# Delta-rule attention on one Trainium2 core: keys, decays and inverses of all heads in the front, the loop fed by one stream of products

## The chip, the cores and the metric

The kernel runs on one core of a Trainium2 chip, in float32. A core has five engines that run side by side, each with its own queue of instructions in a fixed order: TensorE (PE, with its weight loads PEld), VectorE (DVE), ScalarE (ACT), GpSimd (POOL) and SyncE (SP, which here only issues DMAs; ACT and POOL issue some too). The metric is the device time of one execution in microseconds (us), as the median of several runs. Lower is better.

## The reference, cut to what matters

Two layers work on x of 2 sequences x 1024 tokens x 512 channels. Only the first layer's attention is changed:

```python
xn = _layernorm(x)
q = silu(causal_dwconv(xn @ Wq, 4 taps)); k = ...Wk * 128**-0.5; v = ...Wv   # 16 heads of 128
alpha = sigmoid(xn @ Wa + ba); beta = sigmoid(xn @ Wb + bb)                  # one a head and token
# for each token, S is 128x128 for each head and sequence:
#   err = S k - v;  S = alpha * S - beta * err k^T;  o = S q
o = layernorm(o) * ln_w + ln_b
s = (o * sigmoid(xn @ Wg)) @ Wo
g = silu(ternary_swiglu(xn))
x = x + s * g
# second layer: a gated linear recurrence and an FFN of 4-bit weights, in the same manner
```

## The kernel before

**Tiling.** The recurrence over tokens is done in chunks of 128 tokens (NC = 8 a sequence). The 16 heads x 2 sequences make 32 streams, in 8 head groups (`hg`) of 4 streams (2 heads x 2 sequences). A unit is one chunk of one head group: 64 units in all, in the order of `units`: unit u is group 2(u // 16) + u % 2 and chunk (u % 16) // 2, so two groups are worked on side by side, and four such pairs of groups follow one another. The projections q, k, v and gate are made by pieces of two chunks (`p`, 4 a head group).

**Inside a chunk** the delta rule needs the inverse of a triangular matrix of 128 x 128 for each stream. Its diagonal blocks of 32 x 32 are inverted for a whole head group at once by `invert` (L836): blocks of all chunks and streams lie across the 128 partitions, and 31 steps of two tensor_tensor operations follow (`tl` the product, `ml` the subtraction), each on 31 to 256 elements a partition. The blocks come from and go to DRAM (`dl`, loads and stores on SP).

**Stages of `first_layer` (L311).**
1. Layernorm of the 16 token tiles and their transposes (xnT). The ternary FFN is a generator, `mlp()`, with 48 steps; `some(n)` takes n steps of it wherever it is called, so that its matmuls fill gaps.
2. The front, a Python loop over head groups 0 to 3 and their pieces. For each piece: `piece_k().direct` (projection of k by 8 matmuls 128x512, then the three later taps of the convolution as DVE operations with a halo of 3 tokens kept by POOL, and Silu on ACT), `ahead_e` (decays: rows loaded by DMA, a mask on DVE, exponentials on ACT, `e`), `ell()`, which calls `ahead_l` (matmuls `pkk` = k k^T, weighted with e on DVE to `lt`, eight small DMAs a piece to `dl`), and some steps of `invert` for the group before (groups 0 and 1 here). `x_sums` on POOL (`tx`) makes sums of xnT blocks that Strassen-Winograd products need, and two `some(1)` put FFN steps in each piece. The weights of k (`wk`) are loaded on SP at the head of each group.
3. A short prologue: q and v of the first pieces of groups 0 and 1.
4. The loop of 64 units. `weave` (L1240) lays out each unit by hand in 10 slots: in each slot one step of a chain (`across`, the recurrence of this unit and the end of the unit before), whatever `later(n, ...)` has put down for this slot in `due`, and then as many of the `others` as their share of PE work allows: `within` (decays and products inside the next chunk: pqk, kd), `finish` (layernorm of o), and the projections by Winograd with 7 steps a piece where the direct way takes 8, `Piece.step`. The order on each engine in the loop is that written order (`Ordered`, L126). `tasks(u)` (L1199) says which one or two pieces a unit makes: 7 or 14 steps. In the loop before, besides q, v and gate of all groups, k, decays and L of groups 4 to 7 and the inverses (on DVE) of groups 2 to 7 are made, and 11 half output projections (`half`, products `poh`, stored to `pd`).
5. `Join` (L142): the output projection by token tiles (`jpo`, 16 matmuls, or 8 where a half was made), gating with the FFN's output, layernorm, transposes. Then the second layer.

**Pieces in the loop.** After the products of a piece, `Piece.complete` (L730) evicts, adds the ends, applies the bias on ACT (`start`), then three taps for each of two halves on DVE and Silu on ACT. Each of these is put `later` in slots that follow. In `within` (L875) the decays of a unit are loaded to `eb` from DRAM; that tile has one buffer, and the load is issued one slot after the rest.

The front and the stages outside the loop are ordered by a scheduler when the program is built; in the loop the order is as written.

Of the kernel before, what the change touches and what calls it, by code (L numbers as in the profile page):

```python
# [22 lines left out]
P = 128  # L23
# [4 lines left out]
H = 16  # L28
# [113 lines left out]
class Join:  # L142
# [5 lines left out]
    def __init__(self, tc, a, cst, minus_half, od, gd, x1d, pd, room):  # L148
        self.tc, self.a, self.cst, self.minus_half = tc, a, cst, minus_half
        self.room = room.rearrange("p k b t -> p (k b t)")  # L150
        self.od, self.gd, self.x1d, self.pd, self.a = od, gd, x1d, pd, a
        self.ctx = ExitStack()
        self.tp = [self.pool("j_t", 1)]
        self.op = [self.pool("j_o", 1)]
        self.lp = self.pool("j_ln", 3)
        self.wo = []
        self.order = [(c, b) for c in range(NC) for b in range(B)]
        self.o, self.xg, self.made = [], [], 0
        self.load_xg()
# [17 lines left out]
    def load_o(self):  # L177

        n = len(self.o)
        c, b = self.order[n]  # L180
        ot = self.op[n % 3 > 0].tile([P, H, P], F32, tag="ot", name=f"jo_{b * NC + c}")
        h0 = 0
        if n in self.pd:
            h0 = H // 2
            self.tc.nc.sync.dma_start(ot[:, 0:4], self.pd[n].rearrange("p (k t) -> p k t", k=4))
        self.tc.nc.sync.dma_start(
            ot[:, h0:], self.od[c].rearrange("p (h b) t -> p b h t", b=B)[:, b, h0:]
        )
        self.o.append(ot)
# [12 lines left out]
    def product(self, psp, tag, matmul):  # L202
# [9 lines left out]
        h0 = H // 2 if i in self.pd else 0  # L212
        for h in range(h0, H):
            matmul(po, lhsT=ot[:, h, :], rhs=self.wo[h], start=(h == h0), stop=(h == H - 1))  # L214
            if h == H - 1:
# [14 lines left out]
                def gated():  # L230
                    total = po
                    if h0:
                        total = ot[:, 0:4].rearrange("p k t -> p (k t)")
                        nc.vector.tensor_tensor(total, total, po, ALU.add)
                    nc.vector.tensor_tensor(g, total, g, ALU.mult)
# [75 lines left out]
def first_layer(ctx, tc, a, cst, minus_half, keep, xnT, od, gd, pd, then):  # L311
# [32 lines left out]
    early = ctx.enter_context(ExitStack())  # L344
    pa = early.enter_context(tc.tile_pool(name="at_a", bufs=2))
# [165 lines left out]
    pl = early.enter_context(tc.tile_pool(name="at_l", bufs=1, reuse_waits="tile"))  # L511
    wab = pl.tile([P, KC, 2 * H], F32, name="wab")
# [84 lines left out]

    def mm(out, **kw):
        PE.matmul(out, **kw)
# [17 lines left out]
    class Piece:  # L617


        def __init__(self, n, hg, p, dst, after=None):  # L620
# [5 lines left out]
            else:  # L626
                self.pre = pools["p"].tile(
                    [P, 2, B, 2 * P + 4], F32, tag="pre", name=f"pre{self.u}",
                    bufs=3 if "b" in pools else 2,
# [11 lines left out]
        def direct(self, w):  # L641
# [13 lines left out]
            self.complete(0, False)  # L655


        def begin(self, w, x, both, urgent, spare):

            self.w, self.x, self.both, self.urgent = w, x, both, urgent  # L660
            self.engine = POOL if spare else DVE
# [11 lines left out]
        def ended(self):  # L673
            self.left -= 1
            if not self.left:
                self.complete(3 if self.n == "v" else 1, self.urgent)

        def end(self):

            self.ends -= 1  # L680
            if not self.ends:
                ends = self.out[:, 0:4:3]

                def add():
                    self.engine.tensor_tensor(ends, ends, self.both, ALU.add)
# [44 lines left out]
        def complete(self, n, urgent):  # L730
# [32 lines left out]
            if urgent:  # L763
                taps = [lambda a=a, b=b: (a(), b()) for a, b in zip(taps[0::2], taps[1::2])]
            later(
                n,
                lambda: (start(0), kept(), start(1)),
                *taps,
                lambda: (ACT.activation(dst, dst, AF.Silu), self.after()),
            )  # L770
# [40 lines left out]
    def ahead_l(hg, c, store):  # L811

        e, ka = store["es", c // 2][c % 2], store["ka", c // 2]
        k = ka[:, :, (c % 2) * P : (c % 2 + 1) * P]
        assert store["made", c // 2]
        pkk = pools["i"].tile([P, NS, P], F32, tag="pi", name=f"pkk_{hg}_{c}")
# [19 lines left out]
    def invert(hg, store):  # L836
# [14 lines left out]
        for i in range(31):  # L851
# [3 lines left out]
            DVE.tensor_tensor(  # L855
# [6 lines left out]
            DVE.tensor_tensor(rest, rest, tv, ALU.subtract)  # L862
# [12 lines left out]
    def within(hg, c, store):  # L875
# [6 lines left out]
        e = pools["b"].tile([P, NS, P], F32, tag="eb", name=f"eb_{u}", bufs=1)  # L882
# [4 lines left out]
        def block(s):  # L887
# [6 lines left out]
            lambda: nc.sync.dma_start(e, store["e"][c]),  # L894
# [175 lines left out]
    def ell():  # L1070
        if ls:
            hg, p = ls.pop(0)
            for c in (2 * p, 2 * p + 1):
                done(ahead_l(hg, c, stores[hg]))
                if c == 2 * p and hg == 0:
                    some(1)
# [21 lines left out]
    for hg in range(4):  # L1098
        stores[hg] = new_store(hg)
        wk = front_weights(hg)  # L1100
        steps = invert(hg - 1, stores[hg - 1]) if 0 < hg < 3 else iter(())
        for p in range(NP):
            for step in of_e:
                step()
            some(1)
# [3 lines left out]
            of_x = x_sums(n // 4, n // 2 % 2) if n % 2 == 0 else []  # L1109
# [5 lines left out]
            some(1)  # L1115
            ell()
            for _ in zip(range(0 if hg and not p else 14), steps):
                pass
# [6 lines left out]

    tc.keep_in_program_order(nc.vector.tensor_scalar(lnwb, lnwb, 0.5, None, ALU.mult))
# [56 lines left out]
    def piece(n, hg, p):  # L1183

        if n == "k":
            return piece_k(hg, p, stores[hg])
        dst = pools["b"].tile(
            [P, NS, 2 * P], F32, tag=n, name=f"{n}_{hg}_{p}", bufs=3 if n == "gate" else 2
# [4 lines left out]

    def x_of(n, hg, p):

        j = hg // 2 - 2 if n == "k" else hg // 2
        return xs[(NP * j + p) % 2]

    def tasks(u):  # L1199

        j, at = u // 16, u % 16
        p, A, C = at // 4, 2 * j, 2 * j + 1

        def after(hg):
            return (hg, p + 1) if p + 1 < NP else (hg + 2, 0)

        if u >= len(units) - 4:
            return [("gate", (A, C)[at % 4], p)] if u < len(units) - 2 else []
        found = (
            (("k", A + 4, p), ("gate", A, p)),  # L1210
            (("v", *after(A)), ("k", C + 4, p)),
            (("q", *after(A)), ("gate", C, p)),
            (("q", *after(C)), ("v", *after(C))),
        )[at % 4]
        return [t for t in found if t[1] < HG]
# [6 lines left out]
    def woven(pieces, beside):  # L1222

        if beside is none:
            for which, i in ORDER:
                if which < len(pieces):
                    pieces[which].step(i)
                    yield WIDE
        else:
            for i in (None, 0, None, None, 1, 4, None, 5, None, None, 2, 6, None, None, 3):  # L1230
                if i is None:
                    next(beside)
                else:
                    pieces[0].step(i)
                yield WIDE
            done(beside)
# [3 lines left out]
    def weave(chains, others):  # L1240
# [5 lines left out]
        for i in range(LINKS):  # L1246
            order["slot"] += 1
            next(chains[i % 2], None)
            for step in due.pop(order["slot"], ()):
                step()  # L1250
            while given < (i + 1) / LINKS * total:
# [5 lines left out]
    with tc.issue_after(last["act"].ins):  # L1257
        for g in range(2):
            done(step() for step in load_x(g, nc.gpsimd))
        for t in (("q", 0, 0), ("v", 0, 0), ("q", 1, 0), ("v", 1, 0)):  # L1260
            for steps in load_w(*t, nc.gpsimd):
                done(step() for step in steps)
        for i, t in enumerate((("q", 0, 0), ("v", 0, 0), ("q", 1, 0), ("v", 1, 0))):
            one = piece(*t).begin(weights[t], x_of(*t), boths[i % 2], False, True)
            for k in (0, 1, 4, 5, 2, 6, 3):
                one.step(k)
        done(within(0, 0, stores[0]))
        for t in tasks(0):
            for steps in load_w(*t, nc.gpsimd):
                done(step() for step in steps)  # L1270
        halves = sorted(pd)

        class half:


            wo = []

            @classmethod
            def more(cls):
                tag, n = ("e", 2) if cls.wo else ("ka", 2)  # L1280
                for _ in range(n):
                    h0 = len(cls.wo)
                    shape, k = ([P, NS, P + 4], 1) if tag == "e" else ([P, NS, 2 * P], 2)
                    w = pa.tile(shape, F32, tag=tag, name=f"woh_{h0}", bufs=4 if tag == "e" else 2)
                    w = w.rearrange("p s t -> p (s t)")[:, : k * D].rearrange("p (h e) -> p h e", h=k)
                    nc.sync.dma_start(
                        w, a["wo"][h0 * P : (h0 + k) * P, :].rearrange("(h p) e -> p h e", p=P)
                    )
                    cls.wo += [w[:, h, :] for h in range(k)]

            @classmethod
            def load(cls):
                c, b = halves[0] // B, halves[0] % B
                o = pools["w"].tile([P, 7, 2, P], F32, tag="w", name=f"oh_{halves[0]}")
                cls.o = o.rearrange("p k h t -> p (k h) t")[:, 0 : H // 2]
                nc.sync.dma_start(
                    cls.o, od[c].rearrange("p (h b) t -> p b h t", b=B)[:, b, 0 : H // 2]
                )

            @classmethod  # L1300
            def product(cls):
                i, o = halves.pop(0), cls.o
                po = pools["a"].tile([P, D], F32, tag="A", name=f"poh_{i}")

                def out():
                    part = pa.tile([P, NS, P], F32, tag="lt", name=f"part_{i}")
                    part = part.rearrange("p s t -> p (s t)")
                    ACT.copy(part, po)
# [654 lines left out]
```

## Time and profile before

| | us |
|---|---|
| median of 3 runs | 3325.73 (3321.27 to 3327.11) |
| the profiled execution | 3308.21 |
| its span | 3306.4 |
| layernorm, transposes, first FFN steps | 0 to 109 |
| front | 109 to 436 |
| prologue | 436 to 472 |
| loop, first to last unit (a unit begins with the DVE operation `rt`) | 472.5 to 1939.7 |
| output projection and join | 1940 to 2101 |
| second layer | 2101 to 3306 |

Busy over the span: PE 3112.5 us, DVE 2201.2, ACT 1420.0, POOL 1036.7. Times from the profile belong to the profiled execution; the runs' median is 17.5 us longer. A line of a window gives from:to, the length, the busy time and number of instructions of PE, PEld, DVE, ACT and POOL, the granted PE clock (1.00 is full), the busy share of the DMA engines and GB/s. A line of a tile gives line, engine, operation, output<-inputs, count, shortest/median/longest ns, first and last start, and forms (partitions x elements). A float32 matmul leaves two records. In names, the buffer numbers are left out; the timeline gives start, length, engine, line and operation, and in brackets the idle time before it and what ended it; the chain of work gives start, length and what ran. A line of the waits gives who waited for whom: us in total, times, longest.

### The profile page before, as it was taken

To read this page: it belongs to the slowest core of one execution; us is meant where nothing else is said; L and a number is where in the kernel's file an instruction comes from. 1 tells how busy PE (TensorE), PEld (TensorE's weight loads), DVE (VectorE), ACT (ScalarE), POOL (GpSimd) and SP (SyncE) were. 2 spreads that over 40 slices of the span, in tenths; PEclk is the share of its full clock that TensorE was granted. 3 is DMA by queue.
4 is the path that set the end of the run, shared out by engine and by line. 5 is a ranking of instruction groups with operands and counts; after the bars stand their busy time and mean duration, and the time that the engine had idled before them with its cause. 6 is when DMAs were issued, how large, how long until landed. Compare 5 with 4: busy or idle time off the path is not lost. (4 is left out here: it accounts for less than half of the span.)

```text
span 3306.4 us, 41655 instructions
## 1 busy us (share of the span) xinstructions
PE 3112.5 (94%) x13734; PEld 2236.5 (68%) x13734; DVE 2201.2 (67%) x4429; ACT 1420.0 (43%) x2646; POOL 1036.7 (31%) x1286
## 2 busy tenths in 40 slices
PE   8999978988988888899999899999999999999998
PEld 6566757877877777787888864455555555555554
DVE  5566747767677676656666547567667676766677
ACT  3476646655656556444454431132223222322223
POOL 2210053333533334333522222233323333333322
PEclk9999989998999989999999999999999999999999
DMA  7344486665776657565665548201001100011013
GB/s 211 98 139 118 120 253 209 185 190 170 224 217 184 186 171 221 176 189 176 212 181 182 173 140 256 85 32 32 26 26 32 32 26 27 25 39 32 26 35 128
DMA packets 523976, 428.69 MB, mean 130 GB/s; under 512 B 211440, under 2 KB 438512, under 8 KB 523760
## 3 DMA queue, kind: packets, MB, share of 16 engines
q1 hardware_dynamic: 404528, 281.55, 28.7%
q10 hardware_dynamic: 111648, 129.00, 12.6%
q0 software_dynamic: 7584, 15.47, 1.5%
q8 instruction: 110, 1.80, 0.2%
q14 instruction: 106, 0.87, 0.1%
HBM read 291.12 MB, written 122.16 MB: 125 GB/s over the span
## 5 line engine op out<-in xcount | busy, mean ns | idle before, releaser
L134 DVE TENSOR_TENSOR acc<-acc,po 128x512 f32<-128x512 f32 x408 | 278.3, 682 | 208.2 <-PE po L134 207.5
L134 PEld LDWEIGHTS po<-w_d,i 128*128 128x128 f32 x1024 | 194.5, 190 | 142.6 <-issue 110.3
L134 PE MATMUL po<-w_d,i 128*128 128x256 f32 (+1 forms) x1024 | 275.3, 392 | 0.0
L134 ACT COPY g<-pga 128x512 f32<-128x512 f32 x96 | 56.3, 587 | 447.5 <-PE pga L134 437.9
L134 PE MATMUL pga<-xq,w_g 128*128 128x512 f32 x512 | 240.7, 592 | 1.4 <-ACT g L134 1.4
L134 PE MATMUL pua<-xq,w_u 128*128 128x512 f32 x512 | 240.6, 592 | 0.0
L134 ACT ACT_TABLE_LOAD x171 | 219.4, 1283 | 30.5 <-PE pr L134 11.3
L134 POOL TENSOR_TENSOR rs<-rs,minus_half 128x4 f32<-128x4 f32 x64 | 81.7, 1276 | 398.9 <-DVE rs L134 326.2
L134 PEld LDWEIGHTS po<-w_d,s 128*128 128x128 f32 x720 | 136.8, 190 | 95.4 <-issue 77.0
L134 PE MATMUL po<-w_d,s 128*128 128x256 f32 x720 | 184.8, 379 | 0.0
L134 DVE SCALAR_TENSOR_TENSOR v<-prev,cw,v 128x512 f32<-128x512 f32 x192 | 166.6, 872 | 25.2 <-ACT v L134 24.0
L134 POOL TENSOR_TENSOR ot<-ot,gate 128x512 f32<-128x512 f32 x64 | 84.9, 1327 | 303.9 <-ACT ot L134 285.8
L134 DVE SCALAR_TENSOR_TENSOR ka<-prek,cw,ka 128x512 f32<-128x512 f32 x192 | 155.3, 812 | 35.8 <-ACT ka L134 34.2
L134 DVE TENSOR_TENSOR rr<-rr,zw 128x128 f32<-128x128 f32 x192 | 54.9, 286 | 181.3 <-PE zw L134 175.4
L134 PEld LDWEIGHTS pua<-xq,w_u 128*128 128x128 f32 x512 | 96.0, 190 | 76.8 <-issue 72.2
L134 ACT COPY w<-zw 128x128 f32<-128x128 f32 x192 | 51.0, 265 | 225.4 <-PE zw L134 198.0
L134 PE MATMUL paq<-xnT,wq 128*128 128x256 f32 x512 | 137.9, 393 | 10.1 <-ACT preq L134 10.0
L134 PEld LDWEIGHTS pga<-xq,w_g 128*128 128x128 f32 x512 | 97.2, 190 | 72.9 <-issue 66.7
L134 PE MATMUL pagate<-xnT,wgate 128*128 128x256 f32 x512 | 138.3, 395 | 8.7 <-ACT gate L134 8.2
L134 DVE SCALAR_TENSOR_TENSOR q<-preq,cw,q 128x512 f32<-128x512 f32 x192 | 140.2, 746 | 7.0 <-ACT q L134 4.9
L134 ACT ACTIVATE on<-po,nm,rs 128x128 f32<-128x128 f32 x256 | 103.1, 461 | 93.4 <-DVE nm L134 85.7
L134 PE MATMUL pqk<-q,kb 128*128 128x128 f32 x512 | 82.9, 313 | 64.0 <-DVE kd L134 63.6
(284 smaller groups left out, 7856.9 us busy)
## 6 DMA issues: line engine op xcount, KB each, us to landing
wv<-dwv ACTq DMA_DIRECT2D x24, 896.0 KB, 6.2
wq<-dwq ACTq DMA_DIRECT2D x24, 896.0 KB, 6.8
xnT<-dx ACTq DMA_DIRECT2D x42, 512.0 KB, 4.8
wgate<-dwgate ACTq DMA_DIRECT2D x24, 896.0 KB, 6.6
e<-gr SPq DMA_DIRECT2D x64, 256.0 KB, 4.7
de<-e SPq DMA_DIRECT2D x64, 256.0 KB, 3.3
dk<-ka SPq DMA_DIRECT2D x32, 512.0 KB, 3.1
kb<-dk SPq DMA_DIRECT2D x64, 256.0 KB, 3.5
```

Of the source, the lines that this page charges most:

```text
L134: i = getattr(self.engine, name)(*args, **kw)
```

## The change

- The front runs over all 8 head groups (32 pieces). A piece takes one FFN step instead of two (two in every sixth), the x sums come every fourth piece, and the L products alternate between two PSUM pools.
- `invert` gets its engine as an argument. In the front it is GpSimd, for groups 0 to 6, 14 steps at each of the pieces 1 to 3 of the next group. The inverse of group 7 is made on DVE in units 0 to 31, two steps a unit.
- The loop starts at u = −4 and has no k, decays or L. q, v and gate of both groups of a pair come from one stream, `woven()`, of 48 pairs of pieces x 14 steps; units take 10 or 11 steps of it up to unit 57, then 7, 5, 5 and 4. Units −4 to −1 have no chain and take the place of the prologue.
- Taps and Silu go to a list, `put_off`, of which each slot takes one (two if over 14 wait). The adds of the ends are always on POOL.
- `eb` has two buffers and its load is issued at once. q, v, gate and pre have 3, 2, 4 and 4 buffers (2, 2, 3 and 3 before).
- No half output projections: `jpo` has 16 matmuls for every tile. wo is loaded at units 60 and 62.

The diff, cut to its core:

```diff
-    def invert(hg, store):
+    def invert(hg, store, engine):
...
-            DVE.tensor_tensor(
+            engine.tensor_tensor(
                 tv,
...
-            DVE.tensor_tensor(rest, rest, tv, ALU.subtract)
+            engine.tensor_tensor(rest, rest, tv, ALU.subtract)
...
+    put_off = collections.deque()
+
+    def soon(*steps):
+        if order["loop"]:
+            put_off.extend(steps)
+        else:
+            done(step() for step in steps)
...
             taps = [functools.partial(tap, hl, i) for hl in range(2) for i in range(3)]
-            if urgent:
-                taps = [lambda a=a, b=b: (a(), b()) for a, b in zip(taps[0::2], taps[1::2])]
-            later(
-                n,
-                lambda: (start(0), kept(), start(1)),
-                *taps,
-                lambda: (ACT.activation(dst, dst, AF.Silu), self.after()),
-            )
+            taps.append(lambda: (ACT.activation(dst, dst, AF.Silu), self.after()))
+            later(n, lambda: start(0), lambda: (start(1), kept()), lambda: soon(*taps))
...
-        e = pools["b"].tile([P, NS, P], F32, tag="eb", name=f"eb_{u}", bufs=1)
+        e = pools["b"].tile([P, NS, P], F32, tag="eb", name=f"eb_{u}")
+        nc.sync.dma_start(e, store["e"][c])
...
-    for hg in range(4):
+    for hg in range(HG):
         stores[hg] = new_store(hg)
         wk = front_weights(hg)
-        steps = invert(hg - 1, stores[hg - 1]) if 0 < hg < 3 else iter(())
+        steps = invert(hg - 1, stores[hg - 1], nc.gpsimd) if hg else iter(())
         for p in range(NP):
             for step in of_e:
                 step()
-            some(1)
             for step in of_x:
                 step()
             n = hg * NP + p
-            of_x = x_sums(n // 4, n // 2 % 2) if n % 2 == 0 else []
+            of_x = x_sums(n // 8, n // 4 % 2) if n % 4 == 0 else []
             piece_k(hg, p, stores[hg]).direct(wk)
...
             some(1)
+            if n % 6 == 0:
+                some(1)
             ell()
-            for _ in zip(range(0 if hg and not p else 14), steps):
+            for _ in zip(range(14 if p else 0), steps):
                 pass
             ls.append((hg, p))
...
+    pairs = [
+        [(n, 2 * j + i, p) for i in range(2)] for j in range(HG // 2) for p in range(NP) for n in ("q", "v", "gate")
+    ]
+
+    def woven():
+        for i, pair in enumerate(pairs):
+            if i + 1 < len(pairs):
...
+            for n, k in ORDER:
+                pieces[n].step(k)
                 yield WIDE
...
             for step in due.pop(order["slot"], ()):
                 step()
+            for _ in range(min(len(put_off), 1 + (len(put_off) > 14))):
+                put_off.popleft()()
...
-        for u in range(len(units) + 1):
+        steps = invert(HG - 1, stores[HG - 1], DVE)
+        products = woven()
+        for u in range(-4, len(units) + 1):
...
+            if 0 <= u < 32:
+                later(5, lambda: next(steps, None))
+                later(10, lambda: next(steps, None))
...
+            count = {58: 7, 59: 5, 60: 5, 61: 4}.get(u, (10 + turn4 % 2) * (u < 58))
...
-        h0 = H // 2 if i in self.pd else 0
-        for h in range(h0, H):
-            matmul(po, lhsT=ot[:, h, :], rhs=self.wo[h], start=(h == h0), stop=(h == H - 1))
+        for h in range(H):
+            matmul(po, lhsT=ot[:, h, :], rhs=self.wo[h], start=(h == 0), stop=(h == H - 1))
```

## The prediction

> **What bounds the kernel now.** I read the page's busy totals first, then the windows cut at the stage borders, then the chain of waits inside the two stages that change.
>
> ```profile
> PE 3112.5 (94%) x13734; PEld 2236.5 (68%) x13734; DVE 2201.2 (67%) x4429; ACT 1420.0 (43%) x2646; POOL 1036.7 (31%) x1286
> ```
>
> TensorE (PE) carries the kernel; GpSimd (POOL) looks free. The windows (length; busy us of PE, PEld, DVE, ACT, POOL; granted clock) show where PE is not full:
>
> ```profile
> 109.00:436.00 327.00, 317.99 (x1268) 218.22 (x1266) 217.93 (x385) 219.55 (x352) 53.21 (x101) 1.00 0.48 135
> 436.00:472.00 36.00, 28.66 (x124) 23.34 (x124) 13.77 (x21) 14.34 (x29) 20.92 (x33) 0.91 0.91 291
> 472.00:886.00 414.00, 354.64 (x2099) 316.98 (x2100) 287.46 (x676) 246.51 (x507) 157.80 (x213) 0.95 0.64 194
> 886.00:1296.00 410.00, 357.78 (x2133) 321.48 (x2132) 293.45 (x702) 251.94 (x516) 153.87 (x202) 0.95 0.66 196
> 1296.00:1643.00 347.00, 319.96 (x1870) 274.70 (x1869) 224.76 (x612) 162.52 (x362) 134.95 (x160) 0.97 0.63 185
> 1643.00:1940.00 297.00, 280.84 (x1698) 243.31 (x1697) 180.59 (x473) 140.89 (x315) 82.91 (x99) 0.98 0.59 182
> 1940.00:2101.00 161.00, 159.75 (x472) 79.44 (x473) 89.63 (x226) 18.98 (x39) 26.57 (x33) 1.00 0.61 190
> ```
>
> Front (109 to 436) and tail (1940 to 2101): PE 97 and 99% busy at full clock. Loop (472 to 1940, 64 units): PE idle for 414 − 354.6 + 410 − 357.8 + 347 − 320 + 297 − 280.8 = 155 us, and the clock falls to 0.95 where the gaps are. One wait stands for much of it, a decay product behind a DMA with a single buffer (eb):
>
> ```profile
> PE pqk L134 <- DVE kd L134: 63.6, 33, 5.4
> ```
>
> **The loop, part by part.** By timeline starts an f32 128x512 matmul takes 0.86 us (two records), as does a Winograd step. One unit's own chain is 72 records of 128 columns, 8.05 us. Before, units 0 to 31 take 25.7 us each, 32 to 47 21.7, 48 to 62 about 20; where PE never waits (units 37 to 43, 46 to 56) a unit takes its PE work times 1.00 to 1.06. The change takes out k, decays, L, inverses and half projections, and spreads the 672 remaining products (q, v, gate) over units −4 to 61: 10.5 × 0.86 + 8.05 = 17.1 us of PE per unit. DVE then has about 12.7 us a unit (74%), ACT 11, POOL 9: none is the bound, and taps from a list, one a slot, no longer come in bursts ahead of kd. eb gets a second buffer and an early load, so I count the 63.6 us wait as gone; if it stays, it costs 63.6 again. What is late next is the product copies of ACT. Low end 17.1 (PE full), high end 19 (the in-order DVE and ACT stall as in units 48 to 62, 20 us with the same chain); I take 17.6, nearer the full units, since the DVE share is theirs. With 65 us for the last units: 58 × 17.6 + 65 = 1086 against 1467 from first to last unit. **−381.** Units −4 to −1 (42 steps of 0.86, with eviction 40 us) are counted below. The inverse of group 7 stays on DVE in units 0 to 31, two steps (four ops of 0.37 us) a unit, beside PE.
>
> **The tail.** Eleven tiles get back 8 matmuls of 0.86 each. The chain there is pure PE, one tile of 16 records (8 matmuls) after another:
>
> ```profile
> 2050.53 6.87 PE jpo L214 x16
> 2057.40 0.47 PE ptr L117 x4
> ```
>
> So 11 × 6.9 = **+76**. The 11 DVE adds dropped, and the four wo loads placed in units 60 and 62, lie beside PE.
>
> **The front.** PE work alone would be mild: 16 further pieces of eight matmuls (6.9) and pkk (1.8) are 139 us, the k products they replace in the loop are counted out there; PE-bound the front would end at 436 + 139 = 575. SP's share: each moved piece issues 13 DMAs (2 e, 2 de, 1 dk, 8 dl), each group 8 for the inverse, 0.35 to 0.59 us each, some 110 us more in a front of 300 us more: SP is not full, only its order matters. But seven inverses now go to POOL. Each is 31 steps of two ops that hang on each other, 176 elements a partition on average:
>
> ```profile
> L134 DVE TENSOR_TENSOR tl<-ll,ml x248: 180/368/1508, 236.8 to 1603.1; 128x31 f32<-128x31 f32 x8, 128x87 f32<-128x87 f32 x8, 128x135 f32<-128x135 f32 x8, 128x175 f32<-128x175 f32 x8
> L134 DVE TENSOR_TENSOR ml<-ml,tl x248: 183/376/1376, 237.0 to 1603.3; 128x31 f32<-128x31 f32 x8, 128x87 f32<-128x87 f32 x8, 128x135 f32<-128x135 f32 x8, 128x175 f32<-128x175 f32 x8
> ```
>
> On DVE that is 62 × 0.37 = 23 us. POOL's nearest op is the x sum, 256 elements, two SBUF inputs (start, length):
>
> ```profile
> 125.96 1.18 POOL L1090 TENSOR_TENSOR tx<-xnT 128x256 f32<-128x256 f32 x1 [38.36 <-DVE sp_sp_e L102]
> ...
> 131.70 0.72 POOL L1088 TENSOR_TENSOR tx<-xnT 128x256 f32<-128x256 f32 x1
> ```
>
> 0.72 us by itself; other POOL sums of 512 take 1.09, so 176 elements come to 0.60 us, and P, one inverse on POOL, to 62 × 0.60 = 37 us. The 1.18 us beside DVE's hd says that the two engines hold each other up (factor 1.6). The same shows on DVE:
>
> ```profile
> L134 DVE SCALAR_TENSOR_TENSOR ka<-prek,cw,ka x192: 652/747/1656, 115.8 to 1267.1; 128x512 f32<-128x512 f32 x192
> ```
>
> A k tap is 0.75 us alone, 1.10 to 1.17 beside a POOL sum in the front. So P lies between 23 (DVE's speed) and 59 (every op times 1.6); I take **50**, since about 37 DVE ops with two SBUF inputs (taps, masks, hd/hl) fall beside each inverse and the front's DVE is 67% busy.
> The Trainium skill's page "SBUF — State Buffer" (section "SBUF: two separate sides") calls the port pair of both engines an exclusive lock, held for the whole instruction, for a DVE op with two SBUF inputs against a GpSimd op that reads SBUF. It speaks against the move: an estimate by it puts all 37 DVE ops in line, P = 37 + 37 × 0.72 = 64; the change would then cost +120.
>
> Why P is on the path: in the instruction order of the changed kernel the inverse is one POOL block per head group, and the weights of k for groups 2, 4 and 6 stand on SP's queue behind the store (dl<-ll) of the inverse of groups 0, 2 and 4; in the odd groups the margins of the next k pieces (POOL) stand behind the block. POOL's order waits with it for the x sums and loads. So inverses and pieces alternate instead of overlapping. After an even group's inverse: ACT copy 0.7, store 4.5, wk load 4.7, piece 6.9, pkk 1.8 and 0.9, piece 6.9, pkk 1.8, lt 0.7, dl store 3.5, ll load 4.2, and about 4.4 of SP issues (0.43 to 0.59 each) = 41 us until the next inverse starts. After an odd one (weights are there): margin 0.2, identity 1.6, taps 4.5, silu 1.1, piece 6.9, pkk 1.8, lt 0.7, dl 3.5, ll 4.2, issues 4 = 28. The first inverse starts near 218 (236.8 before; some four mlp steps, 5 us each, move behind it). The mlp steps fill PE during these waits but run out in group 5. From the fifth inverse's end: store and weights 10, eight pieces at 8.7 = 70, then, behind the seventh inverse (P), POOL's loads and sums for q, 38: first q product at 218 + 5P + 2 × (41 + 28) + 118 + P = 474 + 6P = 774 with P = 50. Plus 40 us of units −4 to −1, the first unit at 814, before 472.5: **+342**, of which some 200 are PE idle.
>
> **Sum.** Change = (474 + 6P + 40 − 472.5) + (58u + 65 − 1467) + 76 = 6P + 58u − 1284.5, with u the unit: 300 + 1021 − 1284.5 = +36. The page's run took 3308.2 (span 3306.4, 1.8 outside), so 3345 for it; that run is 17.5 us under the median of the runs, 3325.7, so on the median 3362. The second layer (1205 us) is untouched. About 0.2% (7 us) is what a measurement here can tell from no change.
>
> **Rivals.**
> - *GpSimd's inverses are cheap* (P at 37 to 44, 0.26): −71 at P = 37 and u = 17.1, 3255; the sign turns at P = 44 with u = 17.6. For it: POOL is 31% busy, and the extension to 1.18 us is seen in a part of the sums only. Against: the handoffs of 69 us a pair remain. Were they also covered by PE work, the front would end PE-bound at 575 plus 47 for the last inverse, −152: I give that little.
> - *The lock is worse* (P at 58 to 65, 0.18): 6 × 60 puts it at +96, 3422; 65 at +126, 3452. For it: taps up to 1.66 us beside POOL ops.
> - *The loop does not fill PE* (0.10): u = 19 gives +118, 3443: the change then doesn't bring the densest units' rate, since DVE and ACT in order, not eb, held PE back.
> - My forecast (P 44 to 58, u 17.1 to 18.2, 0.46) by itself reaches from −29 to +119: 3297 to 3445.
>
> **How the numbers follow.** The range 3262 to 3452 leaves out the covered front below and the lock with a slow loop above. Faster by over 0.2%: the first rival nearly whole and the lower corner of my case, 0.28; within 0.2%: 0.05; slower: 0.67.
>
> **What would show it.** In the changed profile: tl and ml on POOL at 0.6 to 0.9 us, 45 to 55 us a group; k taps in the front near 1 us; PE idle of some 200 us between 236 and the first q product near 774, and PE waiting for wk at groups 2, 4, 6; units of 17 to 18 us at a clock of 0.98 or more; pqk no longer waiting for kd; jpo one stretch of some 237 us. If the first q product comes before 700, or units take 19 us or more, I am wrong.

## The result, and the profile after

The changed kernel takes 3445.41 us (median of 4 runs, 3440.12 to 3451.63) against 3326.42 for the kernel before: a ratio of 1.036, 95% interval 1.0333 to 1.0387, or +119 us. The forecast was 3362 in a range of 3262 to 3452. The sign held, but the forecast change of +36 us was less than a third of the measured one. The profiled execution has a span of 3438.3 us against 3306.4.

The page's busy totals and the windows of the kernel after, cut at its own stage borders (front in three parts, prologue, loop in three parts, tail; columns as before):

```profile
PE 3126.3 (91%) x13542; PEld 2192.0 (64%) x13542; DVE 2074.3 (60%) x3948; ACT 1329.4 (39%) x2529; POOL 1289.3 (37%) x1704
```

```profile
214.00:438.00 224.00, 172.58 (x649) 116.48 (x647) 106.69 (x141) 112.25 (x192) 124.58 (x225) 0.88 0.42 112
438.00:640.00 202.00, 133.85 (x505) 89.30 (x506) 76.31 (x106) 92.61 (x162) 84.83 (x170) 0.83 0.44 108
640.00:802.00 162.00, 87.59 (x273) 48.06 (x272) 60.36 (x83) 64.34 (x120) 80.72 (x164) 0.75 0.47 132
802.00:856.00 54.00, 44.73 (x175) 37.08 (x176) 22.01 (x29) 21.33 (x42) 28.74 (x41) 0.83 0.78 256
856.00:1444.00 588.00, 548.21 (x3497) 498.01 (x3496) 410.78 (x1011) 303.21 (x685) 271.01 (x310) 0.99 0.62 188
1444.00:1927.00 483.00, 451.05 (x2916) 413.77 (x2915) 301.42 (x792) 250.92 (x567) 211.29 (x243) 0.99 0.63 188
1927.00:1998.00 71.00, 62.25 (x445) 56.44 (x444) 52.88 (x142) 34.11 (x77) 29.56 (x28) 1.00 0.44 125
1998.00:2234.00 236.00, 236.00 (x653) 113.20 (x652) 84.92 (x216) 18.96 (x39) 26.96 (x33) 1.00 0.50 149
```

PE's work is nearly what it was (3126.3 against 3112.5: 16 k pieces of 8 products instead of 7). So 118 of the 132 us by which the span grew are PE standing, and the standing moved: in the loop the gaps shrank (about 80 us after 155), in the front PE now stands 588 − 394 = 194 us from 214 to 802, no engine there is busy for more than about two thirds, and the clock falls to 0.75. An engine list in which nobody is full suggests work that alternates instead of overlapping. What PE waited for in this stretch (who waited for whom: us in total, times, longest):

```profile
PE pk L135 <- DMA wk<-in_wk: 43.0, 1, 43.0
PE pkk L135 <- ACT prek L135: 42.8, 7, 8.6
PE pg L135 <- ACT sg L135: 35.8, 2, 26.8
PE paq L135 <- DMA wq<-in_wq: 27.7, 1, 27.7
```

Together that is 149 of the 194 us. These are the weights of k, ACT's evictions of k products, the Silu of the FFN steps on ACT, and the weights of q.

| stage | before | after | change | forecast |
|---|---|---|---|---|
| first q product | 441.5 | 801.7 | | 774 |
| first unit (first `rt`) | 472.5 | 856.0 | +383 | +342 |
| first to last unit | 1467.2 | 1142.1 | −325 | −381 |
| last unit to the end of `jpo` | 161.7 | 235.5 | +74 | +76 |
| sum | | | +132 | +36 |

The inverse on GpSimd, the k taps, then the waits of ACT and those of SP before the store of an inverse (L862), both between 214 and 802 us:

```profile
L848 POOL TENSOR_TENSOR tl<-ll,ml x217: 239/567/1063, 214.6 to 796.6; 128x31 f32<-128x31 f32 x8, 128x87 f32<-128x87 f32 x8, 128x135 f32<-128x135 f32 x8, 128x175 f32<-128x175 f32 x8
L855 POOL TENSOR_TENSOR ml<-ml,tl x217: 251/622/1222, 214.9 to 796.9; 128x31 f32<-128x31 f32 x8, 128x87 f32<-128x87 f32 x8, 128x135 f32<-128x135 f32 x8, 128x175 f32<-128x175 f32 x8
```

```profile
L135 DVE SCALAR_TENSOR_TENSOR ka<-prek,cw,ka x192: 652/752/1217, 117.0 to 759.6; 128x512 f32<-128x512 f32 x192
```

```profile
ACT ll L135 <- POOL ml L855: 95.6, 17, 11.4
ACT prek L135 <- PE pk L135: 61.2, 28, 6.0
ACT ll L135 <- POOL e L135: 45.6, 5, 11.3
```

```profile
SPq L862 <- ACT prek L135: 33.0, 2, 17.1
SPq L862 <- ACT ll L135: 23.5, 2, 19.1
...
SPq L862 <- ACT g L135: 14.5, 1, 14.5
```

GpSimd does an op in about 0.6 us, as worked out, and the taps are hardly longer than before. The seven inverses span 42.9, 41.7, 42.4, 42.1, 44.9, 40.0 and 39.3 us (first start 214.6, last end 797.2). But from one's end to the next one's start it takes 53.0, 47.0, 54.8, 46.3, 45.1 and 43.4 us, where 41 and 28 were forecast. The waits of ACT tell what was missed: `ll<-ml`, ACT's four copies of an inverse, stand in ACT's fixed order ahead of other work, and ACT waits for GpSimd there for 95.6 + 45.6 = 141 us. SP stands 71 us before the stores.

### The profile page after: what moved, and what is told of

It is laid out like the page before. It is cut to its first block, busy times and chain, and to the rows that moved or that the text cites. A ratio compares the mean times of both kernels' runs of the same rounds, so it can differ in the third digit from the quotient of the medians.

```text
span 3438.3 us, 41084 instructions
## 1 busy us (share of the span) xinstructions
PE 3126.3 (91%) x13542; PEld 2192.0 (64%) x13542; DVE 2074.3 (60%) x3948; ACT 1329.4 (39%) x2529; POOL 1289.3 (37%) x1704
## 4 chain that ended last, share of the span: by engine, by line
PE 61%; DMA 7%; DVE 4%; POOL 3%; ACT 2%; issue 2%; SPq 1%; ACTq 1%; DVEq 0%; POOLq 0%
PE po L135 14%; PE pua L135 6%; PE pga L135 6%; PE jpo L208 5%; PE puc L135 3%; PE pgc L135 3%; PE zw L135 3%; PE pav L135 2%; PE paq L135 2%; PE pxgate L135 2%; PE pagate L135 2%; PE pub L135 2%; PE pgb L135 2%; PE pxv L135 1%; DMA wt<-w 1%
## 5 line engine op out<-in xcount | busy, mean ns | idle before, releaser
L135 PE MATMUL pk<-xnT,wk 128*128 128x512 f32 x512 | 239.7, 620 | 71.1 <-DMA wk<-in_wk 43.0
L135 DVE SCALAR_TENSOR_TENSOR ka<-prek,cw,ka 128x512 f32<-128x512 f32 x192 | 147.7, 787 | 129.2 <-ACT ka L135 98.5
L135 PEld LDWEIGHTS pk<-xnT,wk 128*128 128x128 f32 x512 | 99.7, 199 | 187.7 <-issue 154.3
L135 DVE SCALAR_TENSOR_TENSOR q<-preq,cw,q 128x512 f32<-128x512 f32 x192 | 185.6, 972 | 2.1 <-ACT q L135 0.8
L135 PE MATMUL paq<-xnT,wq 128*128 128x256 f32 x512 | 137.9, 396 | 51.5 <-DMA wq<-in_wq 27.7
L208 PE MATMUL jpo<-xnT,jo 128*128 128x512 f32 x416 | 181.0, 592 | 0.0
```

Of the source, the lines that this page charges most:

```text
L135: i = getattr(self.engine, name)(*args, **kw)
L208: matmul(po, lhsT=ot[:, h, :], rhs=self.wo[h], start=(h == 0), stop=(h == H - 1))
```

## The experiments

Times of stages are from the profiled execution of each; where no ratio is given, the time in all is that of one execution. On the same chips the kernel before took 3319.6 (1 to 4) and 3319.1 us (5 to 8). Run 8, which leaves the front as it is, has its first q product at 800.8 us instead of 801.7. The loop is less steady: in the nine runs with the same loop (after, 1 to 7 and 9) it takes 1142 to 1164 us from first to last unit.

**1. Without the inverse's length** (30 of 31 steps left out in the front):

```diff
-        for i in range(31):
+        for i in range(31 if order["loop"] else 1):
```

> Leaves out 30 of the 31 steps of the inverses of groups 0 to 6 (the output is not the reference's), all else as after. Measured after: seven inverses of 42 us (span) on GpSimd, 43 to 55 us between one's end and the next one's start, first q product at 801.7 us. Theory A (inverse and pieces alternate, each inverse's length lies on the path): P falls from 42 to about 2, the first q product comes near 575 to 600, where TensorE's work alone (466 us from 109) ends, and the execution falls from 3440 to some 3230. Theory B (the front is held by its own order of DMAs, copies and FFN steps, the inverse is hidden): the first q product stays over 740.

Measured: first q product at 671.8 us, 3315.0 us in all (before: 3319.6). Both theories miss: leaving out the inverses, 293 us in all, is worth 130 us, so less than half of their length lies on the path, and PE still stands for 80 us between 214 and the first q product. And even at no cost of GpSimd the change would only have come out level with before.

**2. The inverses on DVE:**

```diff
-        steps = invert(hg - 1, stores[hg - 1], nc.gpsimd) if hg else iter(())
+        steps = invert(hg - 1, stores[hg - 1], nc.vector) if hg else iter(())
```

> The inverses of groups 0 to 6 on DVE instead of GpSimd, all else as after. Theory A (alternation): what counts is the span of an inverse, which was 36 to 40 us on DVE in the front of before against 42 on GpSimd now, so the first q product moves from 801.7 by 6 x 4 = 24 us to about 775, the time by as much. Theory C (GpSimd's slowness is the cause): the ops fall from 0.59 to 0.34 us, the front gets near TensorE's bound, first q product before 680, execution under 3320.

Measured: first q product at 707.5, 3363.5 us. Between the two: 94 us earlier than after. The seven spans add up to 253 us instead of 293 (−40), but the six gaps also fall, from 290 to 238 (−52). The spans on DVE are still 26 to 44 us, though its ops take 0.34 us each. So the engine counts, but not by its ops alone: the handoffs got shorter too, and the first q product no longer waits for the seventh inverse (it comes 10.8 us before its end; in the kernel after it came 4.5 us behind it).

**3. The k weights ahead of the inverse's store:**

```diff
-        wk = front_weights(hg)
+        wk, of_wk = of_wk, None
...
+            if p == 0 and hg + 1 < HG:
+                of_wk = front_weights(hg + 1)
```

> The k weights of the next group are asked for one group earlier in the program, so that on SP's queue the load stands ahead of the inverse's store (dl<-ll) and not behind it; all else as after. If the weights behind the store are the gate after even groups: store 4.5, load 4.7 and copy 0.7 leave three handoffs, perhaps the piece of 6.9 too: 30 to 50 us less until the first q product (801.7), handoffs of 54 us fall to some 40. Rival (the last two L blocks of a group, stored behind the same dl<-ll store on SP, and ACT's copies of ll, are the gate): under 12 us.

Measured: first q product at 778.3 (−23), 3423.5 us; gaps 44.4, 43.8, 45.5, 47.9, 37.8, 44.3. The gaps after groups 0, 2 and 4 lose 7 to 9 us each: store and load, and nothing of the piece. The weights are one gate, and a small one: less than the 30 to 50 us of the theory, more than the rival's 12. Taking away the 43 us for which PE waited for them gave 23, since PE then waited longer behind ACT's prek (73.2 us instead of 42.8). The gaps after even groups are now about those after odd ones. The timeline of this kernel at the end of the second inverse (345.3 us), first ACT, then SP, then PE, shows what holds (start, length, what ran, and in brackets the idle time before it):

```profile
345.37 0.62 ACT L135 COPY ll<-ml 128x256 f32<-128x256 f32 x1 [7.44 <-POOL ml L855]
345.81 0.61 ACT L135 COPY prek<-pk 128x512 f32<-128x512 f32 x1
```

```profile
346.02 3.07 SPq L862 DMA_DIRECT2D dl<-ll  x4
349.20 1.79 SPq L795 DMA_DIRECT2D de<-e  x2
```

```profile
346.48 2.08 PE L135 MATMUL pkk<-ka 128*128 128x128 f32 x8 [7.26 <-ACT prek L135]
348.21 0.77 PE L135 MATMUL po<-dwT,hl 128*128 128x512 f32 x1
```

ACT waits 7.44 us for the inverse's last op; the eviction of the next k piece (prek) stands behind that copy, PE's pkk behind the eviction, and so do the FFN steps that were to fill the wait (their Silu is ACT's). SP stores the inverse and only then goes on with the decays and L blocks of the pieces. One finished inverse opens three queues at once: ACT and PE had stood for 7 us before, SP's queue for 12.

**4. The margins on DVE** (zeros, halo copies and the e memset in the front):

```diff
-                    POOL.memset(to, 0.0) if p == 0 else POOL.tensor_copy(to, self.of_halo)
+                    E = POOL if order["loop"] else DVE
+                    E.memset(to, 0.0) if p == 0 else E.tensor_copy(to, self.of_halo)
...
-            POOL.memset(e[:, :, 0:1], 0.0)
+            DVE.memset(e[:, :, 0:1], 0.0)
```

> In the front the margins of the k pieces (halo copies, zeros) and the e memsets are made by DVE instead of GpSimd, so that no piece waits behind the block of 62 inverse ops on GpSimd; all else as after. If that is the gate after odd groups: identity, taps and silu (8 us) leave three handoffs of 46 us, 20 to 40 us less until the first q product. Rival: the pieces then wait for the L stores behind the inverse's store on SP: under 12 us.

Measured: first q product at 799.5 (−2), 3453.5 us. The rival's figure holds: the margins behind GpSimd's block, which the prediction had as the gate after odd groups, are worth nothing here.

**5 and 6. The inverse keeps to one engine and one queue:**

```diff
+        own = nc.sync if order["loop"] else nc.gpsimd
         for bl in range(4):
-            nc.sync.dma_start(
+            own.dma_start(
                 ll[32 * bl : 32 * bl + 32],
...
-            ACT.copy(ll[:, :, i : i + 8].rearrange("p j i -> p i j"), m[:, i : i + 8])
+            copy = ACT.copy if order["loop"] else POOL.tensor_copy
+            copy(ll[:, :, i : i + 8].rearrange("p j i -> p i j"), m[:, i : i + 8])
...
         for bl in range(4):
-            nc.sync.dma_start(
+            own.dma_start(
                 store["l"][:, :, :, SLOT[bl], :].rearrange("c s j i -> (c s) j i"),
```

with the edits of 3 and 4 (the second of the two without 4).

> The inverse of the front keeps to one engine and one queue: its four transposing copies to ll on GpSimd instead of ACT, its loads (ll<-dl) and stores (dl<-ll) issued by GpSimd instead of SP; the k weights asked for one group earlier and the margins on DVE, as in the two runs before. Measured after: ACT stands 95.6 + 45.6 us before ll copies, SP behind the stores. Theory D (the inverse's end gates the pieces through in-order ACT and SP): pieces run on during an inverse, the gap from one inverse's end to the next one's start falls from 43 to 55 us to 12 to 25, the first q product comes at 590 to 660 instead of 801.7, the execution at 3230 to 3300. Rival E (the gap is the pieces' own work, about 40 us of products, taps and DMA issues that L needs): first q product over 740.

> As the run before, but the margins of the k pieces stay on GpSimd, behind the block of inverse ops and now behind its DMA issues too. Theory D with margins harmless (as the margins alone measured, 2 us): within 15 us of the run before. Rival (once ACT and SP are free the margins become the next gate): 40 to 100 us later, since each piece waits for the block again.

Measured: first q product at 669.6 and 674.3 us, executions of 3322.1 and 3326.2 us, with the kernel before at 3319.1. The gaps of run 5 are 18.3, 18.5, 20.5, 18.2, 19.6 and 19.7 us, those of run 6 are 15.6 to 25.6 (mean 18.8). In run 5 ACT no longer waits for the inverse's copies (after: 95.6 + 45.6):

```profile
ACT prek L135 <- PE pk L135: 68.6, 38, 3.6
ACT ka L135 <- DVE ka L135: 36.4, 22, 4.5
ACT L135 <- POOL tl L851: 35.5, 1, 35.5
ACT e L135 <- DVE e L135: 9.1, 6, 3.5
```

Theory D is right on the gate and the gaps (12 to 25); its 590 to 660 for the first q product is missed by 10, its 3230 to 3300 for the execution by 22. With the inverse's full 45.6 to 49 us left in, run 5 takes off as much (132 us) as leaving the inverse out did (130), but with the weights early, 23 us by themselves (run 3). Run 6 is run 3 with only the inverse's copies, loads and stores moved, and comes 104 us before it. The three were moved together, so which of them counts most is not shown. The inverses have grown by 5.7 us each, now that pieces run beside them: 111 of the 192 k taps start during an inverse, after 45, and 68 take over 0.9 us, after 23.

GpSimd now goes from one inverse to the next: it starts at 209, and 7 x 47.6 + 6 x 19.1 = 448 us end at 657. Its order also holds the end of the front. The zeroing of `ground` (which takes the inverses' blocks in the loop) stands in it behind most of the seventh inverse, ACT's next DMA is issued as it ends, and PE's last L product waits for ACT (first GpSimd, then ACT, then PE):

```profile
641.28 3.30 POOL L1136 MEMSET ground<- 128x3840 f32 x1
```

```profile
644.61 0.65 ACTq L887 DMA_DIRECT2D ground<-dl  x1
645.35 1.28 ACT L135 ACT_TABLE_LOAD   x1 [35.51 <-POOL tl L851]
```

```profile
650.64 3.78 PE L135 MATMUL pkk<-ka 128*128 128x128 f32 x16 [40.43 <-ACT ka L135]
```

That one wait (21.9 us in run 6) is half of the 80 us for which PE still stands from 214 to the first q product of run 5.

**7 and 9. The same on DVE** (edits of 6, but ops and copies on DVE; 9 is the same kernel over several executions):

```diff
-            copy = ACT.copy if order["loop"] else POOL.tensor_copy
+            copy = ACT.copy if order["loop"] else DVE.tensor_copy
...
-        steps = invert(hg - 1, stores[hg - 1], nc.gpsimd) if hg else iter(())
+        steps = invert(hg - 1, stores[hg - 1], nc.vector) if hg else iter(())
```

> As the second of these runs (own queue for the inverse's DMAs, weights early, margins on GpSimd), but the inverse's ops and its copies on DVE. If after the gates are gone the engine no longer counts: first q product within 15 us of the first of these runs. If GpSimd's speed still counts: up to 60 us earlier. If DVE's order (taps behind 62 inverse ops) becomes the gate: later.

> The kernel with the inverse's ops, copies on DVE, its DMAs on GpSimd's queue and the weights early, once more and timed: 3274.6 in one execution, against 3319.1 of before beside it. Expected ratio 0.985 to 0.990 to before: its first unit starts at 682.5 (after 856.0), loop and tail as after.

Measured: first q product at 609.4 and 610.2, an execution of 3274.6 and a median of 3283.7 us; ratio to before 0.991 (0.9888 to 0.9931), just over the 0.985 to 0.990 that were expected. The 60 us to run 5 are the most that was named, but they are not simply GpSimd's speed: the sixth inverse ends later than in run 5 (614.4 us for 591.9). Of the 60 us, 23 are there at the L products of the last piece but one (585.3 for 608.2; what gives them was not taken apart); 37 come at the end, where the wait of 40 us is 12.5 and the first q product does not wait for the seventh inverse, which runs from 631 to 682. The window from 214 to the first q product shows a front that PE fills:

```profile
214.00:609.00 395.00, 366.02 (x1420) 237.61 (x1418) 324.83 (x707) 272.29 (x461) 73.91 (x160) 0.97 0.62 169
```

**8. Only the inverse of group 7 from DVE to GpSimd:**

```diff
-        steps = invert(HG - 1, stores[HG - 1], DVE)
+        steps = invert(HG - 1, stores[HG - 1], POOL)
```

> Only the inverse of group 7 in units 0 to 31 moves from DVE to GpSimd, all else as after. Units 2, 6, 10 and 14 took 20.3 to 21.9 us with DVE busy 18 to 21 us of that, against 17.5 to 18 later. If DVE is the bound there: units 0 to 31 (588 us from first to 32nd) lose 10 to 20 us. Rival (the two engines hold each other up, so taps get longer instead): 0 to 10 us more.

Measured: units 0 to 31 in 586.6 us instead of 588.2, 3447.6 us in all. Units 2, 6, 10 and 14 do fall, from 84.0 to 69.1 us together, so DVE was the bound in these; nearly all of it is lost again in others (units 15 and 16 are 3.4 and 4.3 us longer). The same loop took 590 to 602 us for units 0 to 31 in the eight other runs that have it, so a gain of a few us in all can't be excluded.

**10. The loop's loads on SP's queue** (on the kernel of 7):

```diff
-                    loads, more, kept = load_w(*t, nc.scalar)
+                    loads, more, kept = load_w(*t, nc.sync)
...
-                later(1, *load_x(u // 4 + 2, nc.scalar))
+                later(1, *load_x(u // 4 + 2, nc.sync))
```

> As the run before, and in the loop the loads of the q, v, gate weights and of x come from SP's queue instead of ACT's. Measured after: TensorE stood 77 us in the loop, 17 of it (pxq, pxgate) behind ACT copies into xnT that themselves stood behind a DMA (5.8 us in unit 20), 23 behind ACT evictions of products. Theory F (DMA issues that wait in ACT's order hold its evictions): loop of 1150 us from first to last unit falls by 15 to 40. Rival (ACT's own work, 10 to 13 us of an 18 us unit, and DVE's do it): under 5.

Measured: 1115.3 us from first to last unit, against 1164.4 in the kernel of 9 run beside it (−49); 3233.8 us, ratio to before 0.9765 (0.9742 to 0.9787). That is more than theory F allowed; against the 1150 us of run 7, which its 15 to 40 were meant for, it is 35. The medians of the whole differ by 50 us. ACT's waits in the loop, of after and then of this kernel (columns: who waited for whom, us in total, times, longest):

```profile
ACT w L135 <- DMA ground<-dl: 55.8, 14, 6.8
...
ACT preq L135 <- DMA kb<-dk: 18.3, 4, 6.1
```

```profile
ACT w L135 <- DMA ground<-dl: 21.4, 6, 7.7
```

ACT computes no more and no less in both (588 and 587 us); it stood because it had to issue DMAs in its own order, and the copies behind them kept PE. In the kernel of 9 PE waited for them like this:

```profile
PE paq L135 <- ACT preq L135: 21.9, 12, 4.3
...
PE pxgate L135 <- ACT xnT L135: 11.6, 8, 3.2
PE pxq L135 <- ACT xnT L135: 9.6, 5, 5.5
```

In the loop of run 10 the first two are gone and the third is 0.6 us. The loads of inverse blocks (ground<-dl) are still on ACT's queue; no run moves them.

**11 and 12. The inverse of group 6 in the loop as well,** without and with the edit of 10:

```diff
-        steps = invert(HG - 1, stores[HG - 1], DVE)
+        steps = itertools.chain(*(invert(hg, stores[hg], DVE) for hg in (HG - 2, HG - 1)))
...
-            if 0 <= u < 32:
+            if 0 <= u < 44:
```

> As the first of these runs, but the inverse of group 6 leaves the front too: it goes, like that of group 7, in two steps a unit on DVE, one after the other in units 0 to 43. Measured there: 73 us from the first q product to the first unit, for 36 us of products, with DVE in the inverse of group 6. If that inverse holds the evictions: first unit 25 to 40 us earlier (642 to 658), loop longer by 0 to 10, the execution 20 to 35 shorter. Rival (the wait for the q weights, or cold clock, does it): under 10.

> Both of the last two edits: inverse of group 6 in the loop and the loop's loads on SP's queue, on the kernel with the inverses on DVE. The first gave 12 us between the first q product and the first unit (73 to 61), the second 49 us of loop. If they add: first unit near 675, loop near 1115, 10 to 15 us under the second alone, ratio to before 0.972 to 0.975. Rival (with ACT free, DVE's order is the next bound in units 0 to 43, where it now holds two inverses): the loop gives the 12 us back.

Measured: 61 us from the first q product to the first unit instead of 73, loops of 1166.0 and 1121.9, executions of 3279.9 and 3238.0 us, ratios 0.9899 (0.9868 to 0.9929) and 0.9759 (0.9739 to 0.9779). The first unit of run 11 comes at 676.3 us, 7 before that of run 9 and not the 25 to 40 that were expected, so the rival's "under 10" fits; run 12 is 10 us before run 10 there. In the whole time neither can be told from 9 and 10. The wait for the q weights (about 20 us of PE) remains in all of them. The loads on SP's queue are what makes the fastest versions, 2.4% under the kernel before.

## Why the prediction was right and wrong

- **Direction: right; mechanism: right in part.** The loop gains, and the front loses more. PE idle in the front was put at some 200 us and measured 194. Inverses and pieces do run apart for the most part: 45 of the 192 k taps start while an inverse runs, though the inverses fill half of the time (293 of 583 us). But the sum puts the whole length of six inverses on the path, and run 1 shows 130 us for all of them.
- **P, the inverse on GpSimd: too long.** 50 taken, 42 measured, some 36 of ops and 6 of pauses between them. The 0.60 us for an op, from the x sums, was right; the allowance for DVE and GpSimd holding each other up was not, for a reason inside the forecast itself: if they alternate, they seldom meet. Where they meet, the effect is there: 42 inverse ops that overlap a k tap and no other DVE work take 0.26 us more than the quickest of their shape, 266 with no DVE work beside them 0.003. Beside `hd`, which reads one input from PSUM, nine ops take 0.015 us more; the sum of 1.18 us, which the prediction puts down to `hd`, also overlapped a DVE op with two SBUF inputs (`sp_sp_e`). The Trainium skill's page "SBUF — State Buffer" (section "SBUF: two separate sides") gave 64 by the estimate made from it; 42 were measured in this kernel, and 47.6 where pieces do run beside the inverse (run 5). What failed is the count: the estimate lets all 37 DVE ops meet an inverse op.
- **The gaps: too short, and this is the step that failed.** 41 and 28 were summed over the data's path alone, with the FFN steps as cover; 53.0, 47.0, 54.8 and 46.3 were measured, 63 us more in the four. What was left out: ACT's copies of the inverse and SP's store hold what stands behind them until GpSimd has done its part, the FFN steps too. Runs 3 and 6 show it: with copies, loads and stores of the inverse on GpSimd the six gaps fall from 264 us to 113 and the first q product comes 104 us earlier. The named gates were the lesser ones: weights 23 us (run 3), margins 2 (run 4); of PE's waits for the k weights at groups 2, 4 and 6 only one is seen, the 43.0 us at group 6.
- **That the first q product was only 28 us late is luck.** Up to the end of the fifth inverse, five inverses priced 36 us too high hid more than half of the 63 us by which four gaps were priced too low. From there on 118 + P = 168 were forecast, with one inverse; 172 came, made of two inverses (79), two gaps (89) and 4.5. The clock has no term in the sum: PE's own work from 109 to the first q product took 98.8 + 394.0 = 493 us, where 318 (before) + 139 = 457 would be an estimate at full clock; from 214 on the clock was 0.83.
- **The rival "cheap inverses": its condition came true, its outcome did not.** P was 42, under the turning point of 44, and the kernel was slower. A sign that hangs on one term is only as good as the other terms.
- **Units −4 to −1: 54 us instead of 40.** PE is busy for 44.7 of them at a clock of 0.83; the products are worth 36 at 0.86 us a step, and 1.7 are the first unit's own. Why the clock is low there is not settled: in run 1 PE waits 7.3 us for the q weights before it, not 27.7, and the stretch takes 52.0 us, with 44.7 of PE at 0.85.
- **The loop: u = 17.6 taken, (1926.9 − 856.0) / 58 = 18.5 measured,** 50 us, and 6 more in the last units. Of the forecast's error this is the largest part that nothing hid. The wait for eb went as forecast (2.7 us instead of 63.6), and the steady units do run at 17.5 (37 to 39, 41 to 44, 53 to 55). The excess sits in single units of 19 to 26 us. Run 10 shows a cause, DMA issues in ACT's order: with most of them moved a unit takes 18.0, and the loop 27 us less than in this kernel (1115.3 for 1142.1), 49 less than in its neighbour. Run 8 shows another, DVE in units 2, 6, 10 and 14, though little of it comes out in the sum. What is left over 17.6 was not taken apart further. The prediction names ACT's copies of products as the next thing late, but adds nothing for them.
- **The tail: right** (74 for 76).
- **k taps near 1 us: wrong,** 0.752 in the median, as before.

Together: first q product 28, units −4 to −1 14, loop 56, tail −2: 96 us, the difference between +36 and the +132 of the two profiled executions.

## What to carry to other kernels

When a step moves to a slower but idle engine, price not only its ops but everything that hands its result on: a copy or a store of the result on another in-order queue stops that queue until the step is done (141 us of ACT's waits here), and work meant as cover may stand behind it. Give such a step one engine and one queue of its own before asking how fast it is; here that took 104 us off the front, where leaving the step out took 130. Then look at what stands in that engine's order behind the step: here a single zeroing held PE for 40 us (run 5). In the same way, DMAs issued by a busy computing engine are paid in that engine's order: moving loads to the queue that only issues gave 27 to 49 us of the loop here.

## What the runs showed of the hardware

GpSimd's chained small ops (31 to 256 elements a partition, two SBUF inputs, in float32) took 0.55 to 0.61 us on average in the kernel after where DVE took 0.34 (run 2), a ratio of 1.6 to 1.8; back to back they started with about 0.08 us between one's end and the next one's start. On DVE (run 2) the same inverse still spanned 26 to 44 us for 21 to 24 us of ops, with taps and masks in the same order. Such an op beside a k tap on DVE (two SBUF inputs) took 0.26 us longer in the kernel after, and the 42 taps that met inverse ops took 0.89 us on average, the other 150 took 0.76. In the front of the kernel after, where PE waits, the granted clock was 0.75 to 0.88.
